# GpSimd's share of the input products in the lines layer: slots 2, 4 and 6 instead of parts of 3, 5, 6 and 7

## The chip, the cores and the metric

The kernel runs on one core of a Trainium2 chip. A time is the device time of one execution in microseconds (us). The core has five engines that run their own instruction queues in order and meet at semaphores: TensorE (PE in the profile; its weight loads are PEld), VectorE (DVE), ScalarE (ACT), GpSimd (POOL) and SyncE (SP), which here issues the DMA transfers.

## The reference, cut to what matters

Four layers act on 8 images of 48 x 48 positions with 96 channels, each adding its result to its input after a group normalization. Layers 0 and 3 are two-dimensional selective scans, layer 1 is a filtered MLP, and layer 2, called the lines layer in the kernel, scans every row and every column of the image, forwards and backwards: four directions, each with its own weights. In each direction the layer projects the input to 192 channels, applies a causal convolution of four taps and SiLU to get u, and projects u to a step size delta and to the vectors B and C of 16 states. Then, for every channel d and state n, it runs

```
def step(h, inp):
    dA_i, dBu_i, C_i = inp          # exp(delta*A), delta*u*B, C
    h = dA_i * h + dBu_i
    y = jnp.einsum('bdn,bn->bd', h, C_i)
    return (h, y)
```

from h = 0 along each line of 48 positions. The result, plus D·u, is gated with SiLU(z), projected back to 96 channels and added to the image. All arithmetic is in float32.

## The kernel before, in words

The lines layer handles 8 images, 4 directions and 5 blocks of rows (four of 480 steps, one of 384): 160 blocks. A block has 192 x 16 scans to run over its steps. They are laid out as 24 units: 128 partitions hold 32 channels and 4 states; a unit is one such set of 128 scans. A slot holds three units, the channels of one half of the 192 for one group of four states, so there are eight slots (`ORDER` gives half and state group of each: halves 0 in slots 0 to 3, 1 in slots 4 to 7). Two slots make a turn. There are thus four turns per block, here numbered 0 to 3, and turn q owns slots 2q and 2q+1.

For each slot the kernel needs:

- B and C of four states, spread over the partitions by a DMA (`load_bc`, tile `bc`). The slots of the two halves with the same states (0 and 7, 1 and 6, 2 and 5, 3 and 4) share one load;
- delta and delta·u, spread by another DMA (`load_dd`, tile `dd`), one load per half;
- the products delta·u·B of its three units (`make_dbu`, L299), into a `dbu` room for the whole turn;
- if VectorE makes any of these products, a copy of B by ScalarE to PSUM (`copy_b`, L280, tile `ps_b`, a single bank). GpSimd takes B from `bc` in SBUF. Slot 4 uses the copy of slot 3 if that was the last one made;
- the decays exp(delta·A) (`make_da`, L323), by ScalarE, two units to a tile of `ps_da`, of which there are two;
- the scans (L331), by VectorE, two units to an instruction, in place over the products. A turn has three: the first covers units 0 and 1 (both of the even slot), the second units 2 and 3 (one of either slot), the third units 4 and 5;
- the products with C (`make_hc`, L337), by GpSimd, and their sum over the states by TensorE (`reduce`, L357 and L359).

The order of the work is written out by hand. In turn t (with at = 2t) the queues get, in this order:

```
scan(t, 0)
make_hc(t - 1, 1)
make_dbu(at + 2, nc.vector); make_da(t, 1)
make_dbu(at + 2, nc.gpsimd); make_dbu(at + 3, nc.gpsimd)
scan(t, 1)
make_da(t, 2); copy_b(at + 3)
make_dbu(at + 3, nc.vector)
aside(at); make_hc(t, 0); make_da(t + 1, 0)
scan(t, 2)
copy_b(at + 4); aside(at + 1)
```

(calls of `reduce`, `begin` and `finish` are left out). So turn q makes the products of the next turn's two slots: turn 0 those of slots 2 and 3, turn 1 of 4 and 5, turn 2 of 6 and 7, turn 3 of slots 0 and 1 of the next block. `on_pool` says how many of a slot's three units GpSimd makes, counted from the last: with 3 VectorE has no part in it and there is no copy of B.

`aside(slot)` runs what goes beside the scans at fixed slots. For the lines layer `stage1` prepares a later block: at slot 6 the SiLU of the convolution (`s2s3`, L875), at slot 7 the copy of B, C and delta's input (`s5`, L890), at slot 0 the softplus of delta (`s6`, L903), at slot 1 delta·u on GpSimd (`s7`, L499) with its store to DRAM, at slot 2 the SiLU of z (`s8`, L918, tile `zb`). Each of the first, third and last changes ScalarE's function table twice. `done` makes the gated product (L931, VectorE) after the last reduction of a half; one slot later `project` (L940, TensorE) and then `add` (L946, L948, VectorE) put the block's result into x. The guest is layer 1, which runs image by image in the gaps at slots 0, 2, 3 and 6 with matmuls on TensorE and evacuations on ScalarE (lines from L1113 on).

Of the kernel before, what the change touches and what calls it, by code (L numbers as in the profile page):

```python
# [44 lines left out]
CH = 96  # L45

ON_POOL_SS = {2: 1, 3: 3, 5: 1, 6: 1, 7: 3}
ON_POOL_L2 = {3: 2, 5: 3, 6: 1, 7: 3}


DIRS_SS = [(False, False), (True, False), (False, True), (True, True)]
# [50 lines left out]
def vss_stack_kernel(ctx: ExitStack, tc: tile.TileContext, i: dict, out: bass.AP):  # L102
# [670 lines left out]
    def lines(xin, xout, guest):  # L773
# [208 lines left out]
        guest.rate = 0.42  # L982
        scans(dirs, range(NK), True, ON_POOL_L2, a, pools, ps, stage1, opening, done, side, tail, guest=guest)
        stack.close()
# [365 lines left out]
```

## Time and profile before

| What | Value |
|---|---|
| Median of 3 runs | 17465.54 us (17463.9 to 17466.38) |
| Profiled execution | 17467.17 us, span 17465.4 us |
| VectorE busy | 15969.0 us, 91% |
| GpSimd busy | 15179.8 us, 87% |
| ScalarE busy | 13903.6 us, 80% |
| TensorE busy | 13240.6 us, 76% |
| Mean granted TensorE clock | 0.839 |
| Scans of the lines layer | from 5970.0 to 11900.2 us of the span |

The page gives busy time, share of the span and number of instructions per engine, and then tenths of busy time in 40 slices of 437 us. A row of groups has line, engine, operation, tiles written and read, shapes, the number of instructions, busy time and mean ns of one, and after the bar the idle time of the engine just before them with what ended it. A row of waits has who waited for whom: total us, times, longest. A row of a timeline has start, duration, engine, line, operation, tiles, shapes and number, with an idle time before it in brackets. Consecutive instructions on VectorE and ScalarE overlap by somewhat under 0.1 us, so the time from start to start is shorter than the duration. The share of an engine over the span mixes layers of different balance; the change concerns one of them.

### The profile page before, as it was taken

Reading aid. Unit: us, or ns where it says so; the run is one execution under the profiler, and the core shown is the slowest. Engines: PE = TensorE matmul, PEld = TensorE weight load, DVE = VectorE, ACT = ScalarE, POOL = GpSimd, SP = SyncE. Lnnn points to the kernel's source line nnn. Section 1 sums busy time; section 2 is a strip of 40 time slices with the busy share of each in tenths; the row PEclk is TensorE's granted clock in tenths of the full one; section 3 lists DMA queues with packets and bytes.
Section 4 is the critical chain, followed back from the end, with each engine's and each line's share of the span. In section 5 each row is a group of like instructions: output and inputs, shape, how many; then the busy total and the mean of one; then the engine's idle time right before and its main releaser. Section 6 shows DMA issues by size and latency. Waiting matters only on the chain.

```text
span 17465.4 us, 168933 instructions
## 1 busy us (share of the span) xinstructions
PE 13240.6 (76%) x53740; PEld 4749.1 (27%) x53740; DVE 15969.0 (91%) x9976; ACT 13903.6 (80%) x20972; POOL 15179.8 (87%) x8015
## 2 busy tenths in 40 slices
PE   6778787878787677777777777776777777777776
PEld 1223232333232333233233322222222222222221
DVE  7999999999999799899889999996999999999998
ACT  6878878878787688888788888886878878878776
POOL 7988888988888788888788888886999999999998
PEclk7878888888897888899889888887878878878877
DMA  4554555454555444444444444443555555455454
GB/s 139 179 169 167 174 166 175 169 177 168 165 176 172 135 147 162 147 158 156 153 154 155 153 155 156 153 157 125 173 174 171 176 168 178 171 170 177 169 177 145
DMA packets 887918, 2843.65 MB, mean 163 GB/s; under 512 B 353468, under 2 KB 421788, under 8 KB 760206
## 3 DMA queue, kind: packets, MB, share of 16 engines
q1 hardware_dynamic: 887022, 2832.85, 47.7%
q8 instruction: 422, 6.91, 0.2%
q14 instruction: 474, 3.88, 0.1%
HBM read 2384.40 MB, written 448.17 MB: 162 GB/s over the span
## 4 chain that ended last, share of the span: by engine, by line
DVE 22%; ACT 21%; POOL 19%; issue 14%; PE 13%; DMA 10%; SPq 1%; POOLq 0%; DVEq 0%; ACTq 0%
DVE dbu L331 14%; POOL dbu L337 12%; ACT ps_da L323 7%; DVE dbu L299 6%; POOL dbu L299 5%; DMA dd<-dds 4%; DMA dd<-dd 3%; ACT L323 3%; PE ps_y L357 2%; POOL dds L499 2%; ACT ps_b L280 1%; PE ps_sa L940 1%; PE ps_sa L885 1%; DMA bc<-bcd 1%; ACT L903 1%
## 5 line engine op out<-in xcount | busy, mean ns | idle before, releaser
L331 DVE TENSOR_TENSOR_SCAN dbu<-ps_da,dbu 128x968 f32<-128x968 f32 (+3 forms) x5760 | 11825.2, 2075 | 770.4 <-ACT ps_da L323 610.2
L337 POOL TENSOR_TENSOR dbu<-dbu,bc 128x1440 f32<-128x1440 f32 (+1 forms) x3840 | 10064.7, 2633 | 1941.7 <-DVE dbu L331 1860.2
L323 ACT ACTIVATE ps_da<-dd,w_l_a 128x484 f32<-128x484 f32 (+3 forms) x11520 | 7426.2, 649 | 2436.5 <-DVE dbu L331 2202.9
L357 PE MATMUL ps_y<-dbu,w_red 128*32 128x480 f32 (+1 forms) x23040 | 4253.3, 658 | 1600.6 <-POOL dbu L337 1572.4
L359 PE MATMUL ps_y<-dbu,w_red 128*32 128x480 f32 (+1 forms) x7680 | 4215.2, 657 | 0.0
L299 DVE TENSOR_TENSOR dbu<-dd,ps_b 128x962 f32<-128x962 f32 (+5 forms) x2880 | 3831.5, 1330 | 265.6 <-ACT ps_b L280 156.1
L299 POOL TENSOR_TENSOR dbu<-dd,bc 128x481 f32<-128x481 f32 (+5 forms) x2240 | 3911.2, 1761 | 23.6 <-DMA dd<-dd 19.0
L357 PEld LDWEIGHTS ps_y<-dbu,w_red 128*32 128x32 f32 x23040 | 729.0, 118 | 5033.5 <-POOL dbu L337 3369.4
L280 ACT COPY ps_b<-bc 128x482 f32<-128x482 f32 (+3 forms) x2720 | 1449.2, 533 | 214.7 <-DVE dbu L299 167.3
L574 PE MATMUL ps_side<-xpad,w_l_cw 128*128 128x480 f32 (+1 forms) x2880 | 1342.0, 604 | 48.4 <-ACT g_room L1176 16.9
L323 ACT ACT_TABLE_LOAD x993 | 1274.0, 1283 | 17.8
L703 PE MATMUL ps_s<-bcl,square 128*128 128x480 f32 (+1 forms) x1280 | 888.0, 785 | 323.2 <-ACT dds L707 163.8
L353 PE MATMUL ps_y<-big,eye 128*128 128x480 f32 (+1 forms) x960 | 748.3, 868 | 231.8 <-ACT big L754 227.4
L713 PE MATMUL ps_s<-big,square 128*128 128x480 f32 (+1 forms) x1280 | 849.4, 794 | 65.4 <-ACT g_room L1176 18.5
L499 POOL TENSOR_TENSOR dds<-dds,big 96x960 f32<-96x960 f32 (+1 forms) x320 | 705.9, 2206 | 166.6 <-ACT dds L731 166.2
L574 PEld LDWEIGHTS ps_side<-xpad,w_l_cw 128*128 128x128 f32 x2880 | 570.4, 209 | 804.9 <-issue 696.6
L885 PE MATMUL ps_sa<-ub,square 128*128 128x480 f32 (+1 forms) x640 | 405.0, 770 | 382.9 <-ACT ub L875 382.9
L359 PEld LDWEIGHTS ps_y<-dbu,w_red 128*32 128x32 f32 x7680 | 666.7, 118 | 0.0
L866 PE MATMUL ps_sb<-xpad,square 128*128 128x480 f32 (+1 forms) x1280 | 600.5, 615 | 85.0 <-ACT g_room L1176 31.3
L866 PE MATMUL ps_sa<-xpad,square 128*128 128x480 f32 (+1 forms) x1280 | 538.0, 561 | 0.0
L707 ACT ACTIVATE dds<-ps_s,w_l_dtb 96x480 f32<-96x480 f32 (+1 forms) x640 | 405.1, 633 | 123.4 <-DMA dd<-dds 71.0
L754 ACT COPY big<-ps_y 96x480 f32<-96x480 f32 (+1 forms) x640 | 471.0, 736 | 34.7 <-PE ps_y L359 33.3
(243 smaller groups left out, 12648.2 us busy)
## 6 DMA issues: line engine op xcount, KB each, us to landing
dd<-dd SPq DMA_DIRECT2D x512, 1452.0 KB
bc<-bcd SPq DMA_DIRECT2D x1536, 480.0 KB
dd<-dd SPq DMA_DIRECT2D x256, 1440.0 KB
dd<-dds SPq DMA_DIRECT2D x512, 363.0 KB
dd<-dd SPq DMA_DIRECT2D x128, 1164.0 KB
bc<-bcd SPq DMA_DIRECT2D x384, 384.0 KB
dd<-dds SPq DMA_DIRECT2D x256, 360.0 KB
dd<-dd SPq DMA_DIRECT2D x64, 1152.0 KB
```

Of the source, the lines that this page charges most:

```text
L280: nc.scalar.copy(bps[t][:, :bcs[t][0].shape[1]], bcs[t][0])
L299: engine.tensor_mul(o, du, by.unsqueeze(1).to_broadcast([P, hi - lo, by.shape[1]]))
L323: nc.scalar.activation(da[:, at:at + b.m], b.got[half][:, u % 3, 0, :], AF.Exp, scale=a[:, b.k, ci:ci + 1])
L331: nc.vector.tensor_tensor_scan(db, da, db, 0.0, ALU.mult, ALU.add)
L337: nc.gpsimd.tensor_mul(h, h, bcs.pop(2 * t + sub)[1].unsqueeze(1).to_broadcast([P, 3, n]))
L357: nc.tensor.matmul(y[32 * g:32 * g + 32, :n], lhsT=wc["red"][:, :32], rhs=hc[:, g, b.at], start=False, stop=(slot == 3))
L359: nc.tensor.matmul(y[DH:, :n], lhsT=wc["red"][:, 32:], rhs=hc[:, 2, b.at], start=False, stop=(slot == 3))
L499: nc.gpsimd.tensor_mul(du, dt, u)
L574: nc.tensor.matmul(pu[:, :n], lhsT=flat[:, at:at + P], rhs=xpad[:, r0 + dy:r0 + dy + nr, dx:dx + W], start=(tap == 0), stop=(tap == 8))
L703: nc.tensor.matmul(got["p"][:, :n], lhsT=wide("dtw", (2 * b.k + half) * DH), rhs=b.bcl[:, :n], start=True, stop=True)
L713: nc.tensor.matmul(got["p"][:, :n], lhsT=wide("xp", (2 * b.k + half) * NBC), rhs=uall[:, half], start=(half == 0), stop=(half == 1))
L866: nc.tensor.matmul(got["u", half][:, :n], lhsT=wide("cw", at), rhs=shifted(off), start=(tap == 0), stop=(tap == 3))
```

## The change

One constant is different: the number of units of each slot that GpSimd makes in the lines layer. It is nine of 24 in both versions. The two scan layers have their own table, `ON_POOL_SS`, which is as it was.

```diff
-ON_POOL_L2 = {3: 2, 5: 3, 6: 1, 7: 3}
+ON_POOL_L2 = {2: 3, 4: 3, 6: 3}
```

What each turn issues follows from it (units of products on VectorE and on GpSimd, and the slots whose B ScalarE copies, in the order of its queue):

| Turn | VectorE before | after | GpSimd before | after | Copies before | after |
|---|---|---|---|---|---|---|
| 0 | 3 of slot 2, 1 of slot 3 | 3 of slot 3 | 2 of slot 3 | 3 of slot 2 | 3 | 3 |
| 1 | 3 of slot 4 | 3 of slot 5 | 3 of slot 5 | 3 of slot 4 | 6 | 5 |
| 2 | 2 of slot 6 | 3 of slot 7 | 1 of slot 6, 3 of slot 7 | 3 of slot 6 | next 0 | 7, next 0 |
| 3 | 3 of slot 0, 3 of slot 1 | the same | none | none | next 1, next 2 | next 1 |

VectorE's product in turns 0 to 2 moves from between the first and the second scan to between the second and the third (turn 0 had one in both places). GpSimd's products in these turns are those of the slot that the first scan of the next turn reads; before they were those of the odd slot and, in turn 2, one unit of the even one.

## The prediction

> Names: a block is 480 (or 384) sequence steps of one image and direction; it has four turns, 0 to 3, and eight slots; turn q owns slots 2q and 2q+1 and has three scans. A "product" is delta·u·B (L299), a "readout" h·C (L337).
>
> **What bounds the kernel now.** I read the page's engine totals first.
>
> ```profile
> PE 13240.6 (76%) x53740; PEld 4749.1 (27%) x53740; DVE 15969.0 (91%) x9976; ACT 13903.6 (80%) x20972; POOL 15179.8 (87%) x8015
> ...
> DVE  7999999999999799899889999996999999999998
> ```
>
> VectorE leads, but slices 14 to 27, where the lines layer lies, show gaps. The windows view of that stretch (the gated products of L931 start and stop there; columns PE, PEld, DVE, ACT, POOL, clock, DMA share, GB/s):
>
> ```profile
> 5980.00:11960.00 5980.00, 4538.91 (x18300) 1728.46 (x18300) 5421.80 (x3485) 4894.59 (x7146) 4935.99 (x2254) 0.87 0.43 153
> ```
>
> VectorE idles 558 of 5980 us, 3.5 us per block (160 blocks). The waits of the same stretch (us in total, times, longest):
>
> ```profile
> DVE dbu L331 <- ACT ps_da L323: 255.8, 243, 2.7
> ...
> DVE x L948 <- PE ps_sa L940: 118.7, 99, 2.4
> ...
> ACT ps_b L280 <- DVE dbu L299: 82.6, 147, 3.8
> ```
>
> Groups of 6500 to 11500 us, shapes apart (busy us, mean ns | idle before):
>
> ```profile
> L299 DVE TENSOR_TENSOR dbu<-dd,ps_b 128x1440 f32<-128x1440 f32 x428 | 697.5, 1630 | 40.2 <-DMA dd<-dd 37.0 <-ACT ps_da L323 2.1 <-ACT ps_b L280 0.8
> L299 POOL TENSOR_TENSOR dbu<-dd,bc 128x1440 f32<-128x1440 f32 x214 | 585.7, 2737 | 0.0
> L299 DVE TENSOR_TENSOR dbu<-dd,ps_b 128x960 f32<-128x960 f32 x107 | 120.5, 1126 | 0.0
> L299 DVE TENSOR_TENSOR dbu<-dd,ps_b 128x480 f32<-128x480 f32 x107 | 67.3, 629 | 0.0
> ```
>
> Last, the timeline of a typical block: VectorE turns 0 to 3, then ScalarE.
>
> ```profile
> 8215.58 2.16 DVE L331 TENSOR_TENSOR_SCAN dbu<-ps_da,dbu 128x960 f32<-128x960 f32 x1
> 8217.65 1.63 DVE L299 TENSOR_TENSOR dbu<-dd,ps_b 128x1440 f32<-128x1440 f32 x1
> ...
> 8225.21 2.16 DVE L331 TENSOR_TENSOR_SCAN dbu<-ps_da,dbu 128x960 f32<-128x960 f32 x1 [0.71 <-ACT ps_da L323]
> ...
> 8234.78 1.01 DVE L948 TENSOR_TENSOR x<-x,ps_sa 96x480 f32<-96x480 f32 x1 [1.75 <-PE ps_sa L940]
> 8235.71 2.14 DVE L331 TENSOR_TENSOR_SCAN dbu<-ps_da,dbu 128x960 f32<-128x960 f32 x1
> 8237.77 1.12 DVE L299 TENSOR_TENSOR dbu<-dd,ps_b 128x960 f32<-128x960 f32 x1
> ...
> 8243.47 2.14 DVE L331 TENSOR_TENSOR_SCAN dbu<-ps_da,dbu 128x960 f32<-128x960 f32 x1
> ```
>
> ```profile
> 8215.48 0.54 ACT L280 COPY ps_b<-bc 128x480 f32<-128x480 f32 x1
> ...
> 8216.86 2.64 ACT L323 ACTIVATE ps_da<-dd,w_l_a 128x480 f32<-128x480 f32 x4
> 8219.44 0.54 ACT L280 COPY ps_b<-bc 128x480 f32<-128x480 f32 x1
> 8220.00 1.28 ACT L903 ACT_TABLE_LOAD   x1
> ...
> 8227.40 1.36 ACT L323 ACTIVATE ps_da<-dd,w_l_a 128x480 f32<-128x480 f32 x2 [0.49 <-DVE dbu L331]
> 8228.78 1.28 ACT L918 ACT_TABLE_LOAD   x1
> ```
>
> Each turn has its own bound. Counting every block of the timeline: the scan that opens turn 1 waits over 0.5 us for ScalarE in 144 of 160 blocks, 1.15 us on average, so **turn 0** ends on ScalarE (decays, a copy, table load, two softplus, table load, decay). **Turn 1** ends on the addition to x, which waits 1.02 us for the projection (L940) on average. **Turn 2** is VectorE alone: in over four fifths of the 480-step blocks it lasts 7.77 to 7.78 us, as here (8243.47 less 8235.71). **Turn 3** is VectorE's plus a wait for the dd load (46.8 us in all). The means are 10.20, 9.51, 7.72 and 9.66 us.
>
> [...]
>
> **The change part by part.** It touches the lines layer only. Units on VectorE in turns 0 to 3 go from 4, 3, 2, 6 to 3, 3, 3, 6; on GpSimd from 2, 3, 4, 0 to 3, 3, 3, 0.
>
> *Engine work.* VectorE has five products of three units in place of four, one of two and one of one. Ends overlap the next start, so one costs 1.55, 1.05 or 0.55 us start to start: 7.80 becomes 7.75, a gain of 0.05 us per block. GpSimd loses one instruction of about 0.18 us (1886 − 1034 = 852 ns per unit). Copies of B (L280) stay five: that of slot 2 (end of turn 3) and of slot 6 (end of turn 1) go, slots 5 and 7 get one. The sum matters little; places matter.
>
> *Turn 0, −0.24 us.* VectorE does 0.55 us less, but that becomes waiting, as ScalarE sets the end. ScalarE gains the copy of slot 2 at 8215.48 (0.49 us start to start) where nothing else holds it. After it the first decays of turn 0 would be done early, and the second pair is then held by the end of the first scan (8217.65 plus 0.11) instead of starting at 8218.16: −0.40 here. In 66 of 156 blocks ScalarE waits at that place 0.5 us or more for a guest matmul, and the gain is nothing. Block by block this averages −0.24.
>
> *Turn 1, +0.31.* The copy of slot 5 now stands between the decays of 8227.40 and the table load of 8228.78: 0.48 us on the path to zb, projection and addition. In 84 of 156 blocks L940 starts under 0.48 us after zb is read, mostly at once, and the addition (or the next decays) slips with it; in the others, this one too, TensorE is behind for other reasons and covers it. Average +0.23. The cover lost between first and second scan adds 0.08: with no product there, decays that finish after the first scan (25 blocks, 0.13 us per block) now stall VectorE, partly hidden by the addition's wait.
>
> *Turn 2, +0.56.* Two units become three: 1.55 − 1.05 = 0.50, 0.48 averaged with the short blocks. Lost cover costs 0.13 (37 blocks in which the second decays would end after the first scan, even less the 0.49 us of slot 6's copy). Turns already over the floor give back 0.05.
>
> *Turn 3, −0.21.* VectorE arrives later at its first product, and dd was late there in 49 blocks; the wait shrinks by that.
>
> Slot 3, 5 and 7's products wait for their copies: scan end + 0.11 + 1.30 + 0.54 = 1.95 us, against a second scan of 2.07. Covered by 0.1 us; uncovered it would cost at most that per turn.
>
> *GpSimd's new deadline.* Its product now has to be ready for the first scan of the next turn, not the second. Queue from turn 0's start: readout 2.7, product 5.4, readout 8.1, du (L499) and memset 10.1, readout 12.8, product 15.5, readout 18.2, readout 20.9, product 23.6. First scans that need them: 9.3, about 19 and 27.3. Slack is 3.5 us or more, so its cost is zero; GpSimd's readouts come no later than now. DMA issues keep number and order; du, which starts the dd store, leaves GpSimd about 0.6 us earlier.
>
> *Sum.* −0.24 + 0.31 + 0.56 − 0.21 = +0.42 us per block, × 160 = +67 us. The profiled execution took 17467.2 us (span 17465.4), 1.6 over the median; 17465.5 + 67 = 17532. Bounds: turn 0 from −0.5 to 0, turn 1 from 0 to +0.5, turn 2 from +0.3 to +0.7, turn 3 from −0.3 to 0; not all at one end, so +0.25 to +0.75, 17505 to 17585.
>
> **The rivals.** *No difference (0.22).* The later arrivals are swallowed: turn 1's copy finds TensorE late everywhere (0), turn 0 gains 0.35, turn 2 costs 0.5. +0.1 per block, 17480. For it: 72 of 156 blocks have that cover; against: the late blocks, where no guest runs, have none.
>
> *Faster (0.10).* The copy of slot 3 waits now for VectorE's product of slot 2, because ps_b is one bank; 82.6 us of such waits stand above. If these sit in turn 0 they go, 0.52 per block, and with the copy of slot 2 (0.49) and turn 3 (0.2) the gain is 1.2 against 0.9 of cost in turns 1 and 2: −0.3 × 160, 17417. It decides once turn 0 shortens by over 0.9. Against: most of those waits are of slot 1's copy, in turn 3, which stays.
>
> *GpSimd late (0.08).* If its product ends after the first scan is due, VectorE stalls in three turns: past the slack of 3.5 us each microsecond costs 3 × 160 = 480 us. A stall of 0.3 us beyond it gives 17676. GpSimd's idle 1.6 us per turn (5980 − 4936 over 640 turns) speak against it.
>
> **How the numbers follow.** The case worked out has 0.60, no difference 0.22, faster 0.10, GpSimd late 0.08. A difference of 0.2%, 35 us, is about what a measurement here can tell. Slower 0.68, same 0.22, faster 0.10. The range 17450 to 17600 leaves out most of the faster case and the late GpSimd.
>
> **What would show it.** Turn 2's floor at 8.3 us instead of 7.8; turn 0 shorter by 0.2 to 0.4 with a longer wait at turn 1's first scan than 1.15 us; zb about 0.5 us later within turn 1 and more waiting of L946/L948; no first scan waiting for POOL L299. Wrong if turn 2 does not lengthen, if turn 0 shortens by VectorE's full 0.55, or if scans wait for GpSimd.

## The result and the profile after

The changed kernel takes 17585.28 us (median of 6 runs, 17579.14 to 17595.43), against 17465.96 us for the kernel before (6 runs): a ratio of 1.0066, 95% interval 1.0053 to 1.0079. That is 119 us more, inside the forecast range and on the side that it held likelier, but 52 us more than the 67 that the sum gave. The profiled execution took 17581.87 us, 114.7 more than that of before.

The page's totals for the kernel after, then its row of 40 slices for VectorE and the group of L885 (the projection of u to delta's input, B and C):

```profile
PE 13315.0 (76%) x53740; PEld 4785.1 (27%) x53740; DVE 15963.2 (91%) x9816; ACT 13913.7 (79%) x20972; POOL 15165.5 (86%) x7855
...
DVE  7999999999999789888888899996999999999998
...
L885 PE MATMUL ps_sa<-ub,square 128*128 128x480 f32 (+1 forms) x640 | 435.4, 822 | 497.2 <-ACT ub L875 497.2
```

VectorE's busy time has hardly moved (15969.0 before), and only the lines layer's slices have become emptier. Beside it stands a row that the prediction did not look at: the change does not touch L885, but one of its instructions now takes 822 ns in place of 770, and TensorE idles 497.2 us ahead of them in place of 382.9. The same row of the kernel before, from its page:

```profile
L885 PE MATMUL ps_sa<-ub,square 128*128 128x480 f32 (+1 forms) x640 | 405.0, 770 | 382.9 <-ACT ub L875 382.9
```

The windows view of the lines layer after, from 5980 us to the end of its scans (columns PE, PEld, VectorE, ScalarE, GpSimd, clock, DMA share, GB/s), answers to the one shown in the prediction:

```profile
5980.00:12012.00 6032.00, 4582.56 (x18238) 1746.30 (x18236) 5413.73 (x3310) 4897.72 (x7132) 4889.22 (x2076) 0.87 0.43 151
```

The scans of before end at 11900.2 us and these at 12011.6; over 5980 to 11900 us VectorE was busy 5413.83 us before. So the layer ends 111 us later and VectorE works as long as it did: **all of the loss is VectorE's waiting**. The waits view of that stretch after:

```profile
DVE dbu L331 <- ACT ps_da L323: 378.9, 333, 4.2
...
DVE x L948 <- PE ps_sa L940: 117.2, 94, 2.8
...
ACT ps_b L280 <- DVE dbu L299: 62.5, 236, 4.1
...
DVE dbu L331 <- POOL dds L502: 33.2, 44, 1.4
...
DVE dbu L299 <- DMA dd<-dd: 14.7, 14, 3.8
```

Scans wait 123 us more for decays (255.8 before), products 32 us less for the dd load (46.8 before), and the addition to x waits as it did; ScalarE's copies of B wait less for VectorE (82.6 before) and more often. The row with L502, a memset of GpSimd, is a matter of attribution: in all 44 cases ScalarE's decays for the same scan end 0.10 us before it starts, and no row has a scan waiting for GpSimd's products. Sorting VectorE's waits by the place in the block says more (us over the layer's 160 blocks, counted instruction by instruction from both traces):

| VectorE waits before | before | after |
|---|---|---|
| turn 0, second scan | 30.3 | 185.5 |
| turn 1, first scan | 183.7 | 146.8 |
| turn 1, second scan | 5.6 | 18.9 |
| turn 1, addition to x (L946, L948) | 163.0 | 162.4 |
| turn 2, first scan | 8.7 | 19.6 |
| turn 2, second scan | 2.5 | 19.7 |
| turn 3, product that needs dd | 46.8 | 14.7 |
| gated product (L931) | 19.2 | 5.1 |

The differences add up to 113 us, of which the first row alone makes 155. In turn lengths (start of the first scan to the next turn's, mean of 156 blocks), turns 0 to 3 went from 10.20, 9.51, 7.72 and 9.66 us to 10.42, 9.70, 8.24 and 9.42. Turn 0, which should have become shorter, is 0.22 us longer.

Here is the timeline of VectorE in the block that the prediction showed, after:

```profile
8267.75 2.16 DVE L331 TENSOR_TENSOR_SCAN dbu<-ps_da,dbu 128x960 f32<-128x960 f32 x1 [1.94 <-ACT ps_da L323]
8269.82 1.63 DVE L299 TENSOR_TENSOR dbu<-dd,ps_b 128x1440 f32<-128x1440 f32 x1
...
8284.44 1.01 DVE L948 TENSOR_TENSOR x<-x,ps_sa 96x480 f32<-96x480 f32 x1 [1.86 <-PE ps_sa L940]
8285.36 4.20 DVE L331 TENSOR_TENSOR_SCAN dbu<-ps_da,dbu 128x960 f32<-128x960 f32 x2
8289.47 1.63 DVE L299 TENSOR_TENSOR dbu<-dd,ps_b 128x1440 f32<-128x1440 f32 x1
...
8293.63 2.15 DVE L331 TENSOR_TENSOR_SCAN dbu<-ps_da,dbu 128x960 f32<-128x960 f32 x1
```

Turn 2 is 8293.63 less 8285.36, 8.27 us: the floor of 8.3 as forecast. (A row with x2 joins two scans that follow each other.) In turn 0 the first scan starts at 8263.65, right behind the last of turn 3, and the second, which was to follow it, waits 1.94 us for its decays. ScalarE's timeline after, at that moment, shows what held them:

```profile
8265.45 0.55 ACT L1193 COPY g_room<-ps_sb 48x480 f32<-48x480 f32 x1 [1.84 <-PE ps_sb L1196]
8265.91 0.55 ACT L890 COPY bcl<-ps_sa 38x480 f32<-38x480 f32 x1
8266.36 2.64 ACT L323 ACTIVATE ps_da<-dd,w_l_a 128x480 f32<-128x480 f32 x4
```

ScalarE idles 1.84 us for a matmul of the guest (L1196), evacuates it, copies `bcl` out of the bank of L885, and only then comes to the decays, 2.71 us into the turn; before it was 1.28 us (8216.86 less 8215.58). TensorE's timeline, first before, then after, shows why that matmul is late:

```profile
8209.57 0.57 PE L359 MATMUL ps_y<-dbu,w_red 128*32 128x480 f32 x1
8212.92 1.88 PE L885 MATMUL ps_sa<-ub,square 128*128 128x480 f32 x4 [2.79 <-ACT ub L875]
8214.73 1.01 PE L1196 MATMUL ps_sb<-g_room,g_downt 73*48 73x480 f32 x2
```

```profile
8256.98 0.57 PE L359 MATMUL ps_y<-dbu,w_red 128*32 128x480 f32 x1
8260.99 3.49 PE L885 MATMUL ps_sa<-ub,square 128*128 128x480 f32 x4 [3.44 <-ACT ub L875]
8264.41 1.01 PE L1196 MATMUL ps_sb<-g_room,g_downt 73*48 73x480 f32 x2
```

Against the start of turn 0, L885 starts where it did (2.66 us ahead), since it waits for ScalarE's SiLU. But the reductions of turn 2 that stand before it on TensorE's queue ended 0.66 us earlier, so TensorE idled 3.44 us instead of 2.79, and the four instructions of L885 (two matmuls) took 3.49 us instead of 1.88. The windows view from the start of L885 on, 2.70 us of each kernel, before and then after, gives the reason in its clock column (third from the end):

```profile
8212.90:8215.60 2.70, 2.67 (x6) 0.84 (x6) 2.56 (x3) 2.66 (x4) 1.76 (x2) 1.00 0.00 0
```

```profile
8260.98:8263.68 2.70, 2.69 (x4) 1.18 (x4) 2.56 (x3) 2.59 (x3) 1.82 (x2) 0.50 0.03 11
```

The granted clock was 1.00 before and is 0.50 after. Both traces record every stretch of constant clock, 1518 before and 1610 after: the clock is 1.00 and 0.50 in turn, and each stretch begins on a grid of 3.413 us, to within 1 ns. A window is from here on one step of this grid. The windows view, cut on it, has just ahead of L885 and after it, first before and then after (TensorE's busy time is the second number of a row):

```profile
8211.01:8214.42 3.41, 1.50 (x4) 0.68 (x4) 3.41 (x3) 3.37 (x5) 2.52 (x1) 1.00 0.04 16
8214.42:8217.84 3.42, 2.14 (x5) 0.65 (x5) 3.28 (x3) 3.35 (x7) 2.48 (x2) 1.00 0.01 3
```

```profile
8257.44:8260.85 3.41, 0.11 (x4) 0.00 (x0) 3.41 (x3) 3.20 (x5) 0.82 (x1) 1.00 0.67 266
8260.85:8264.27 3.42, 3.28 (x4) 1.18 (x4) 3.28 (x3) 2.70 (x4) 2.54 (x2) 0.50 0.03 11
```

Before, TensorE was busy for 1.50 of 3.41 us and the next window ran at full clock; after, for 0.11 us, and the next ran at half. Counted over all windows from 5970 to 11900 us of each trace that ran at full clock, the clock of the next one goes with this busy share:

| TensorE busy in the window | windows before | next one at half clock | windows after | next one at half clock |
|---|---|---|---|---|
| under 40% | 172 | 172 | 207 | 207 |
| 40 to 50% | 96 | 60 | 74 | 43 |
| 50 to 75% | 352 | 17 | 312 | 22 |
| over 75% | 687 | 0 | 685 | 1 |

So gaps shorter than a window came with half clock, and their length alone did not decide: in the kernel after, L885 ran at half clock at 7923.68 us (3.57 us for the four) behind a gap of 3.11 us, of which 2.36 lay in one window, and at full clock at 6572.95 us (1.88 us) behind one of 3.50 us, of which 1.80 lay in one window and 1.70 in the next. Of 156 blocks 86 ran L885 and what follows it mostly at half clock before, with an idle gap of 2.39 us on average (382.9 us over 160 blocks); 119 do so after, with 3.11 us. Before, the gap touched a window that was busy under 40% in 74 blocks, after in 111, and all of these ran at half clock.

### The profile page after: what moved, and what is told of

The parts are those of the page before. It is cut to its first block, busy times and chain, and to the rows that moved or that the text cites. A ratio compares the mean times of both kernels' runs of the same rounds, so it can differ in the third digit from the quotient of the medians.

```text
span 17580.1 us, 168519 instructions
## 1 busy us (share of the span) xinstructions
PE 13315.0 (76%) x53740; PEld 4785.1 (27%) x53740; DVE 15963.2 (91%) x9816; ACT 13913.7 (79%) x20972; POOL 15165.5 (86%) x7855
## 4 chain that ended last, share of the span: by engine, by line
DVE 17%; ACT 13%; POOL 13%; issue 10%; PE 8%; DMA 5%; SPq 0%; POOLq 0%; DVEq 0%; ACTq 0%
DVE dbu L331 11%; POOL dbu L337 8%; DVE dbu L299 5%; ACT ps_da L323 4%; POOL dbu L299 3%; DMA dd<-dds 3%; ACT L323 2%; PE ps_sa L885 2%; DMA dd<-dd 2%; POOL dds L499 2%; PE ps_sa L940 1%; ACT ps_b L280 1%; ACT L903 1%; ACT L875 1%; PE ps_y L357 1%
## 5 line engine op out<-in xcount | busy, mean ns | idle before, releaser
L299 DVE TENSOR_TENSOR dbu<-dd,ps_b 128x962 f32<-128x962 f32 (+5 forms) x2720 | 3809.0, 1400 | 230.2 <-ACT ps_b L280 155.7
L299 POOL TENSOR_TENSOR dbu<-dd,bc 128x481 f32<-128x481 f32 (+3 forms) x2080 | 3890.0, 1883 | 21.8 <-DMA dd<-dd 18.9
L885 PE MATMUL ps_sa<-ub,square 128*128 128x480 f32 (+1 forms) x640 | 435.4, 822 | 497.2 <-ACT ub L875 497.2
L866 PE MATMUL ps_sb<-xpad,square 128*128 128x480 f32 (+1 forms) x1280 | 603.4, 618 | 77.9 <-ACT g_room L1176 32.1
```

The costliest lines, as they stand in the source:

```text
L299: engine.tensor_mul(o, du, by.unsqueeze(1).to_broadcast([P, hi - lo, by.shape[1]]))
L866: nc.tensor.matmul(got["u", half][:, :n], lhsT=wide("cw", at), rhs=shifted(off), start=(tap == 0), stop=(tap == 3))
```

## The experiments

**Theory**: turn 2, as changed, makes GpSimd's readouts earlier (it makes three units there instead of four, and the second scan no longer stands behind a product of VectorE), so TensorE idles longer ahead of L885, falls to half clock more often, and ScalarE, which waits for its matmuls, brings turn 0's decays late. **Rival**: the move within turn 0 loses by itself, because with no product of VectorE between the first scans the decays are exposed, and the clock is a bystander. The two are told apart by doing the change turn by turn, and by keeping TensorE busy. None of these kernels leaves out work.

### One turn at a time

Three kernels, each with the edit in one turn only. One turn's edit alone does not keep the nine units on GpSimd: it makes ten with turn 0's, nine with turn 1's and eight with turn 2's.

```diff
-ON_POOL_L2 = {3: 2, 5: 3, 6: 1, 7: 3}
+ON_POOL_L2 = {2: 3, 5: 3, 6: 1, 7: 3}   # turn 0 alone
+ON_POOL_L2 = {3: 2, 4: 3, 6: 1, 7: 3}   # turn 1 alone
+ON_POOL_L2 = {3: 2, 5: 3, 6: 3}         # turn 2 alone
```

> GpSimd makes all of slot 2 in turn 0 (VectorE all of slot 3); slots 5, 6 and 7 as before, so GpSimd has ten units. Turn 0 is as in the changed kernel, turns 1 to 3 as before. Clock theory (TensorE falls to half clock before turn 0 because turn 2's readouts come earlier; turn 2 is as before here, so it does not): the idle time before L885 stays about 2.4 us, turn 0 falls from 10.20 by the 0.2 us of the forecast, total 17425 to 17455. Cover theory (turn 0 grew because no product stands between its first and second scan): turn 0 rises to about 10.4, total 17495 to 17510.

> Only slots 4 and 5 change places; GpSimd has nine units, ScalarE one copy of B more (slot 5). Both theories: turn 1 rises from 9.51 by 0.2 to 0.3 us, the others stay, total 17490 to 17515.

> Only turn 2 changes: GpSimd makes all of slot 6 and none of slot 7, with slots 3 and 5 as before (eight units on GpSimd, sixteen on VectorE). Clock theory: turn 2 rises from 7.72 to about 8.25, the idle time before L885 rises to about 3.1 us, and turn 0, in which nothing is changed, rises by 0.2 to 0.5 us; turn 3 falls by 0.2; total 17540 to 17600. Cover theory: turn 0 stays near 10.2, so +0.5 -0.2 = +0.3 per block, total near 17510.

Measured, with the kernel before at 17479.09 us (18 runs; each series has its own runs of the kernel before, and each ratio is to those; the idle time is the page's total over 160 blocks):

| Kernel | us | ratio (95%) | turn 0 | turn 1 | turn 2 | turn 3 | idle ahead of L885 | blocks at half clock |
|---|---|---|---|---|---|---|---|---|
| before | 17479.09 | | 10.20 | 9.51 | 7.72 | 9.66 | 2.39 | 86 of 156 |
| turn 0 alone | 17430.99 | 0.9972 (0.9960 to 0.9983) | 10.14 | 9.42 | 7.74 | 9.58 | 2.35 | 88 |
| turn 1 alone | 17513.71 | 1.0018 (1.0010 to 1.0027) | 10.23 | 9.71 | 7.74 | 9.61 | 2.48 | 93 |
| turn 2 alone | 17562.90 | 1.0048 (1.0033 to 1.0063) | 10.45 | 9.43 | 8.31 | 9.52 | 3.12 | 119 |

The longer idle gap, most of the added half clock and the longer turn 0 come with turn 2's edit (turn 1's adds 0.03 us to turn 0): it lengthens turn 0, which it does not touch, by 0.25 us. The page's group of L885 shows it at once, first with turn 0's edit alone, then with turn 2's:

```profile
L885 PE MATMUL ps_sa<-ub,square 128*128 128x480 f32 (+1 forms) x640 | 406.3, 773 | 376.1 <-ACT ub L875 376.1
```

```profile
L885 PE MATMUL ps_sa<-ub,square 128*128 128x480 f32 (+1 forms) x640 | 434.6, 820 | 499.4 <-ACT ub L875 499.4
```

773 ns is the value of before (770), 820 that of after (822). The rival has part of the truth: with turn 0's edit alone the wait of turn 0's second scan rises from 30.3 to 140.1 us, and turn 0 gains 0.06 us only. But it is a gain, in the whole kernel too, and not the loss of 0.22 that the full change shows there. In turn 0 the three edits add up to the whole change: −0.06, +0.03 and +0.25 make +0.22.

A fourth kernel has turns 1 and 2 as changed and turn 0 as before (eight units on GpSimd):

```diff
-ON_POOL_L2 = {3: 2, 5: 3, 6: 1, 7: 3}
+ON_POOL_L2 = {3: 2, 4: 3, 6: 3}
```

> The edits of turns 1 and 2 without that of turn 0 (slot 3 keeps two units on GpSimd, eight units in all). Clock theory: with TensorE slow ahead of turn 0, turn 0's edit gains nothing in their company, so the ratio is that of the whole change, 1.006 to 1.007. If the three edits simply add up (alone they made -48, +32 and +84 us), it is 1.0067 too, but the whole change would then be 1.004; so if the ratio here lies above 1.008, turn 0's edit still gains and turns 1 and 2 harm each other instead.

It took 17627.14 us, ratio 1.0082 (1.0067 to 1.0097) against 17480.31 for the kernel before. Turn 0 is 10.54 us, so in the presence of the other two edits that of turn 0 is worth 0.12 us in its own turn (10.42 in the full change). In the whole time the run settles little: its interval overlaps that of the full change (1.0053 to 1.0079) and all but reaches the sum of the single edits of turns 1 and 2 (0.18 and 0.48%, 1.0066).

### TensorE kept busy

The changed kernel with matmuls of zero weights behind the last reduction of turn 2. They add zero to a sum that is still open, and fill a part of the idle time ahead of L885:

```diff
+            if restart and q == 3:
+                for _ in range(6):
+                    nc.tensor.matmul(ys[b, 1][:32, :b.n], lhsT=pools["still"][0], rhs=pools["still"][1][:, :b.n], start=False, stop=False)
```

(A second line, left out here, sets `still` to 32 columns of zeros as weights and a tile of the convolution's weights as data.)

> The changed kernel with six matmuls with zero weights on TensorE in turn 3 of each lines block, between the reduction of turn 2's readouts and L885, where TensorE idles 3.1 us; they add zero to columns of y and hold nothing up. Clock theory: the four L885 take 1.3 to 1.5 us start to start instead of 1.87, ScalarE waits less for the guest's matmuls, turn 0 falls from 10.42 to 9.8 to 10.0, total 17500 to 17530. Cover theory: turn 0 stays at 10.4, total 17580 to 17590.

It took 17641.92 us, ratio 1.0093 (1.0078 to 1.0108): slower still. The clock did what was meant (2 of 156 blocks at half clock), but six were too many. Each matmul is two instructions of some 0.4 us, so L885 started some 1.3 us ahead of turn 0 instead of 2.6, and the delay took the place of the half clock: turn 0 was 10.70 us. Both expectations missed. The run shows that TensorE's lateness costs turn 0 whatever its cause; it does not tell the theory from its rival. The next ones put fewer there: three in the changed kernel, two in the kernel before (whose gap is shorter), and two with turn 0's edit alone.

> The changed kernel with three idle matmuls with zero weights in turn 3 instead of six: each takes two TensorE instructions of 0.4 us, so six held L885 up by 1.3 us, and three (2.4 us) end about 0.9 us before it can start. Clock theory: TensorE stays at full clock there (under a tenth of the blocks slow around turn 0's start, 119 of 156 before), L885 starts 2.67 us ahead of turn 0 as in the changed kernel and its four matmuls take 1.3 us, turn 0 falls from 10.42 to 9.7 to 10.1, and the total is 0.3% to 0.6% below the changed kernel: a ratio to before of 1.000 to 1.004. Cover theory: turn 0 stays at 10.4, ratio 1.006 to 1.007.

> The kernel before with two such matmuls (1.6 us) at the same place, where TensorE idles 2.4 to 2.6 us. Clock theory: the slow clock around turn 0's start, in 86 of 156 blocks before, goes from most of them and turn 0 falls from 10.20 by 0.2 to 0.4 us, ratio 0.996 to 0.998. Cover theory: no difference, ratio 1.000.

> Turn 0's edit alone with two such matmuls. Clock theory: ScalarE's gain of a copy is no longer lost where it waited for TensorE, so turn 0 falls below 9.9 and the ratio is 0.992 to 0.996, under both that of turn 0's edit alone (0.9972) and that of the matmuls alone. Cover theory: as turn 0's edit alone, 0.997.

TensorE's timeline of the changed kernel with three such matmuls (L445; lines are shifted by four, L889 is L885 and L1200 is L1196), same block:

```profile
8208.50 0.57 PE L359 MATMUL ps_y<-dbu,w_red 128*32 128x480 f32 x1
8208.89 2.58 PE L445 MATMUL ps_y<-square 128*32 128x480 f32 x6
8212.51 1.88 PE L889 MATMUL ps_sa<-ub,square 128*128 128x480 f32 x4 [1.05 <-ACT ub L879]
8214.32 1.01 PE L1200 MATMUL ps_sb<-g_room,g_downt 73*48 73x480 f32 x2
```

Turn 0 starts at 8215.17 there: L889 starts 2.66 us ahead of it, as L885 did in the changed kernel, and again takes 1.88 us. Against the kernel before at 17480.31 us (19 runs):

| Kernel | us | ratio (95%) | turn 0 | turn 1 | turn 2 | turn 3 | blocks at half clock | wait of turn 0's second scan |
|---|---|---|---|---|---|---|---|---|
| after, three | 17483.24 | 1.0000 (0.9992 to 1.0009) | 9.74 | 9.73 | 8.24 | 9.42 | 10 of 156 | 70.1 |
| before, two | 17439.42 | 0.9979 (0.9968 to 0.9989) | 9.91 | 9.56 | 7.72 | 9.67 | 16 | 9.8 |
| turn 0 alone, two | 17381.31 | 0.9946 (0.9929 to 0.9962) | 9.73 | 9.44 | 7.71 | 9.60 | 15 | 68.5 |

Adding work to TensorE makes the changed kernel 0.66% faster (1.0066 to 1.0000): its whole loss is gone. Turns 1 to 3 stay as they were to 0.03 us; only turn 0 moves, by 0.68 us. The rival, by which turn 0 would have stayed at 10.4 us, is out. The kernel before gains 0.21% by the same means, so the change costs 0.21% at full clock (37 us, or 44 by the two medians), and the other 0.45% or so of the 0.66 is half clock that it brings (each ratio is known to some 0.1%). And turn 0's edit, at full clock, shortens turn 0 by 0.18 us (9.91 to 9.73), three times what it did at the old clock.

### A second gap of TensorE

The z projection and the one to x, in turns 0 and 1, often run at half clock as well. On top of the last kernel, three zero-weight matmuls go ahead of the z projection, into the bank that it then overwrites:

```diff
+                got["z", 1] = ps("sb", 1)
+                for _ in range(3):
+                    nc.tensor.matmul(got["z", 1][:32, :n], lhsT=pools["still"][0], rhs=pools["still"][1][:, :n], start=True, stop=True)
```

(The rest of the edit, left out here, makes the projection take this bank and not a new one.)

> Turn 0's edit, the two idle matmuls in turn 3, and three more with zero weights ahead of L909 at slot 1, where TensorE waits for the guest and falls to half clock in over half of the blocks until the projection L940 is done. If the half clock sets the wait of the addition to x there too, that wait falls from about 0.95 us per block to 0.3 to 0.5, turn 1 from 9.44 to 8.9 to 9.1, ratio 0.988 to 0.992. If the wait is set by ScalarE (zb) or GpSimd alone, turn 1 stays and the ratio is 0.994 to 0.996.

It took 17351.55 us, ratio 0.9938 (0.9921 to 0.9955) against 17466.19. That is less of a gain than expected, and not clear of the kernel without the three (0.9946, 0.9929 to 0.9962). The waits view of the lines layer, VectorE's rows, for turn 0 alone with two, then with the three more (L952 and L956 are L948 of the kernel before, L944 and L948 its L940):

```profile
DVE x L952 <- PE ps_sa L944: 108.1, 89, 2.3
...
DVE dbu L299 <- DMA dd<-dd: 30.4, 33, 4.0
```

```profile
DVE dbu L299 <- DMA dd<-dd: 70.8, 69, 5.7
...
DVE x L956 <- PE ps_sa L948: 27.3, 32, 3.9
```

The addition's wait in these rows falls by 81 us and turn 1 from 9.44 to 8.84 us. The z projection ran at half clock in 2 of 160 blocks in place of 104, and its instructions took 630 ns in place of 897 (means of the 480-step ones into the first bank), so half clock was behind most of that wait. But the dd load, a DMA, is now waited for 40 us more; turn 3 grows from 9.60 to 9.87, turn 2 from 7.71 to 7.83 and turn 0 from 9.73 to 9.78, and of the 0.60 us per block 0.16 is left. Why the dd load comes later was not followed up.

## Why the prediction was right or wrong

The side and the range were right, and so were turns 2 and 3. Turn 1 was right in sign, but only in part by the path forecast. Turn 0 failed, and is named first.

- **Turn 0, −0.24: wrong, +0.22 measured, outside its bounds of −0.5 to 0.** Two things failed. First, its own term: turn 0's edit alone gave −0.06. The step placed the second decays by ScalarE's queue as it stood in the trace of before, with the guest matmuls where they were. Its own caveat, that ScalarE waits 0.5 us or more for such a matmul in 66 of 156 blocks, was taken as a constant; with turn 0's edit alone there are 84 and after the whole change 105 (62 before by the same count). With TensorE at full clock the term is near its size: −0.18. Second, turn 2's edit adds 0.25 to turn 0, a term that the prediction put at nothing (next point). The wait of the second scan rose by 155 us, 0.97 per block, which exceeds the 0.55 of VectorE's lost work plus the 0.23 by which turn 1's first scan waits less: +0.19. That first scan was forecast to wait longer.
- **"GpSimd's readouts come no later than now", cost zero: the premise held, the conclusion failed.** They come earlier, 0.66 us in the block shown, and an earlier readout was not free: TensorE, which waits behind it for an event that did not move, idled the longer for it (3.44 us instead of 2.79 in that block) and was slower afterwards (3.49 us instead of 1.88 for L885). This is the larger part of turn 0's miss of 0.46, shown by turn 2's edit alone (+0.25 in turn 0) and by the filled gap (turn 0 from 10.42 to 9.74).
- **Turn 1, +0.31: +0.19 measured.** The lost cover was 0.08, as forecast (second scan's wait 5.6 to 18.9 us). The copy of slot 5 did put zb 0.46 us later in the turn, but of the 0.23 that this was to cost, 0.07 shows, at the first scan of turn 2 (8.7 to 19.6 us); the addition to x waits as before. That row was forecast to grow and did not.
- **Turn 2, +0.56: +0.52 measured.** The third unit is there (7.77 to 8.27), and the lost cover is 0.11 per block (2.5 to 19.7 us) against 0.13.
- **Turn 3, −0.21: −0.24 measured.** The wait for dd fell by 32.1 us, 0.20 per block.
- **Copies covered by 0.1 us, GpSimd's slack of 3.5 us, engine work near nothing**: nothing contradicts them. No scan waits for L299 on GpSimd, and VectorE's busy time in the layer is the same. Moving the products lengthened them on neither engine: one of three units took 1630 ns before and 1627 after on VectorE, 2737 and 2736 on GpSimd (480 steps, means from 6500 to 11500 us).
- **The rivals.** No difference is out by the interval, though its premise on turn 1 came near: of the copy's 0.23, 0.07 shows. It failed because turn 0 gave nothing. Faster would have needed turn 0 to give more than 0.9 us; it gave none. Late products of GpSimd did not occur.

By the sum: 0.42 us per block was forecast and 0.69 measured (110 us over 160 blocks, 119 in the medians), the difference being turn 0's 0.46 less 0.19 from the other three. At full clock the four turns of the change are −0.17, +0.17, +0.52 and −0.25, 0.27 us per block. That the range held was luck in part: turn 0 lay outside its own bounds, and turns 1 to 3, each below its forecast, made up for 0.19 of it. Nothing in the range knew of the clock.

Not settled: what decided for windows of which TensorE was busy 40 to 50%, with half clock next in 60 of 96 before and in 43 of 74 after. The ends of matmuls are modelled in the trace, so the busy shares are themselves approximate.

## What to carry to other kernels

"Not later" is not the same as "free": where one engine's work comes earlier and the next engine still waits for a third, its idle time grows. Here TensorE's grew from 2.39 to 3.11 us ahead of L885, and the matmuls that follow ran at half clock in 119 blocks instead of 86. So when a change moves work off TensorE's producers, read the idle time ahead of its next burst and the clock column there, block by block (1.00 before and 0.50 after in the one shown), not the mean over the span (0.839 before, 0.836 after). Where such a gap lies ahead of matmuls that others wait for, a few matmuls of zero weights that end before the burst is due are worth trying, and their number decided here: three recovered 0.66%, six cost 0.27% more.

## What the runs showed of the hardware

- In the traces of before and after the granted TensorE clock took two values only, 1.0 and 0.5, and changed only on a grid of 3.413 us that ran on through the whole execution (1518 stretches before, 1610 after).
- A window at full clock in which TensorE was busy under 40% was followed by half clock in all 379 cases from 5970 to 11900 us of these two traces; one busy over 75% in 1 of 1372.
- Idle gaps ahead of L885 of 2.4 us on average came with half clock in 86 of 156 blocks (before); at 3.1 us it was 119 (after, and turn 2 alone), at 0.8 to 0.9 us 10 to 16 (the three kernels with two or three zero-weight matmuls), at 0.06 us 2 (six).
- The four instructions of L885 took, from the first start to the last, 1.31 us at full and 2.56 us at half clock (480 steps, before and after).
- One float32 matmul of 480 columns was two TensorE instructions: three gave six, in 2.58 us (after, three).
